# A gated attention and mixture-of-experts block on one core: the first batch's softmax in a written-out order over six banks, its values by way of DRAM, and the mixture's transposes moved up

## The chip, the core and the metric

One core of a Trainium2 chip runs the whole program. The metric is the device time of one execution, in microseconds (us). Five engines work side by side, each through its own instruction stream in order: TensorE (PE, matmuls, with its weight loads PEld), VectorE (DVE), ScalarE (ACT), GpSimd (POOL) and SyncE (SP, which issues DMAs). Nothing overtakes within a stream, so an instruction that waits holds up all behind it.

## The reference, cut to what matters

```python
# x: (8, 256, 512), ctx: (8, 256, 512); H = 32 heads of D = 16, HK = 8 key heads
x = x + tanh(g_xattn) * attention(layernorm(x), ctx)
x = x + tanh(g_ffn) * ffn(layernorm(x))

# attention: queries from [ctx, x]; keys and values from ctx and from x, side by side
q  = heads(concat([ctx, xn]) @ Wq);  k = heads(xn @ Wk);  sk = heads(ctx @ Wsk)
scores = q @ concat([sk, k]).T / 4 + alibi;  a window of 64 positions back, else -inf
o = softmax(scores) @ concat([ctx @ Wsv, xn @ Wv]);  return o @ Wo

# ffn: per token a softmax router over 128 experts, the best 4, each a mixture of 8 bases
basis = silu(xt @ w_gate) * (xt @ w_up)            # 8 bases of 256
out   = sum over the 4 experts of coeff * (mix[expert] . basis) @ w_down
out   = out + (silu(xt @ sw_gate) * (xt @ sw_up)) @ sw_down
```

## The kernel before

The eight batches follow each other, two tiles of 128 tokens each, all in float32. For a batch b there are four kinds of work, each a Python generator that records a few instructions and then yields an estimate of their time. `run` (near the end of the kernel) always advances the generator that is due first, so each engine's order is the order of recording.

- `project(b)` normalizes x, transposes it (`tr_x`, copied to `xnT` by ACT) and makes keys (`pk`, L491, copied to `kT` at L498), queries (`pq`, L510, copied to `qT` at L517) and values (`pv`, L530, copied into the padded tile `vpad` at L453). All of these take turns on the one PSUM bank with the tag "one", with `hold` and `give`.
- `diagonals` (L447) spreads `vpad` with 16 DMAs of 128 KB into the block-diagonal tile `vbd`, 2.1 MB in rows of 1 KB, which the matmuls with the softmax's result read.
- `attention(b)` has 16 steps u, two for each of 8 groups i. `score(i)` (L574) makes four score banks; in each step `soften` (DVE, L587) adds the bias and takes the minimum, `exponentials` (ACT, L601) follow, `divide` (reciprocal on DVE at L610, four multiplications on POOL at L613) and `turn` (a DVE transpose into `pt`, L621). After every two groups `values` (L643) multiplies `pt` by `vbd` and `take` (ACT, L660) copies the result to `oT`. `tail(b, t)` then makes the output projection (`po`, L763), the second normalization (`tr_f`) and the router (`pl`, `pst`, `pc`).
- `feed_forward(b)` multiplies ten pieces k (eight bases and two halves of the shared part) by a scheme with seven products of half size (`m`, L896 and L905). For that it needs sums of weight quarters: they are made once (`sub`, L848), stored to DRAM (`keep`, L852) and reloaded for later batches. For k = 0 to 3 `first_weights` makes them ahead of the first batch's feed-forward, on POOL; for the others `feed_forward(0)` makes them as it goes. At the end the mixture `mixed` is transposed (`pm`, L1067), copied (`mT`, L1070) and multiplied by `w_down` (`pd`, L1042).

Before the loops stand the loads and, in `project_first`, batch 0's first keys and queries: context keys, first-half queries, the transposes of x, then second-half queries. The rest of batch 0's projection, the values among it, is recorded by the same generator between steps of `attention(0)`. The setup runs under the framework's own ordering, what follows under the written one:

```python
        start(attention(0), 0.42, at=-0.62, total=74.1)
        start(first, 0.12, at=-0.615, total=7.1)
        start(project(1), 0.54, at=-0.54, total=44.0)
        start(first_weights(), 0.42, at=-0.52, total=25.0)
        start(once(coefficients, *coef_in), 1.0, at=-0.46)
```

Of the kernel before, what the change touches and what calls it, by code (L numbers as in the profile page):

```python
# [32 lines left out]
MASKED = 1e32  # L33


@with_exitstack
def gated_block(
# [38 lines left out]

    turns = [0]
# [15 lines left out]
    def hold():  # L93
        me = object()
        queue.append(me)
        while queue[0] is not me or now[0] < given[0] + GAP:
            yield 0.4
# [8 lines left out]
    def load(b):  # L106
        xt = three.tile([P, NT, HID], F32, tag="x", name=f"x_{b}")
        nc.sync.dma_start(xt, x[b].rearrange("(t p) d -> p t d", p=P))
        return xt

    def load_context(b):

        ctT = one.tile([P, NC, T], F32, tag="shT" if b == 1 else "ctT", name=f"ctT_{b}")
        nc.sync.dma_start(ctT, context_t[b].rearrange("(c p) t -> p c t", p=P))
        return ctT
# [8 lines left out]
    ctT_0 = load_context(0)  # L124
    wsk_sb = weight(wsk, HID, HK * D, "wsk", nc.scalar)
    for t in range(NT):
        nc.sync.dma_start(x_0[:, t, :], x[0, t * P : (t + 1) * P, :])
    loaded[0] = x_0, ctT_0
    wq_sb = const.tile([P, 2 * NC, HID], F32, tag="wq", name="wq")
    for half, eng in enumerate((nc.scalar, nc.sync)):  # L130
        if half:
            wk_sb = weight(wk, HID, HK * D, "wk", nc.scalar)
        eng.dma_start(
            wq_sb[:, half * NC : (half + 1) * NC, :],
            wq[half * HID : (half + 1) * HID].rearrange("(c p) n -> p c n", p=P),
        )
    wsv_sb = weight(wsv, HID, HK * D, "wsv", nc.scalar)
    wv_sb = weight(wv, HID, HK * D, "wv", nc.sync)
    loaded[1] = load(1), load_context(1)


# [3 lines left out]
    nc.gpsimd.memset(neghalf, -0.5)  # L145

# [26 lines left out]
    def transposed(dst, src, t, name, bank):  # L173
# [7 lines left out]
    first_normed = [norm(loaded[0][0], [t], f"a0_{t}")()[0] for t in range(NT)]  # L181

    rows_i = const.tile([P, 1], I32, tag="rows_i", name="rows_i")
    nc.gpsimd.iota(rows_i, pattern=[[0, 1]], base=0, channel_multiplier=1)
    odd_i = const.tile([P, 1], I32, tag="odd_i", name="odd_i")
    nc.vector.tensor_scalar(
        odd_i, rows_i, D, D.bit_length() - 1, op0=ALU.bitwise_and, op1=ALU.logical_shift_right
    )  # L190
    kmask = const.tile([P, 2], F32, tag="kmask", name="kmask")
    nc.vector.tensor_copy(kmask[:, 1:2], odd_i)
    nc.vector.tensor_scalar(
        kmask[:, 0:1], kmask[:, 1:2], -1.0, 1.0, op0=ALU.mult, op1=ALU.add
    )

# [20 lines left out]
    for kv in range(HK):  # L217
        nc.gpsimd.tensor_scalar(
            nbias[:, kv], dist, slope, 2.0 ** (-8.0 * G * kv / H), op0=ALU.mult, op1=ALU.mult
        )  # L220


    vpad = const.tile([P, NT * 2, (2 * HK + 1) * D], F32, tag="vpad", name="vpad")
    nc.gpsimd.memset(vpad.rearrange("p a n -> p (a n)"), 0.0)


    vbd = const.tile([P, P // Q, NT * 2, HK, 2 * D], F32, tag="vbd", name="vbd")

# [22 lines left out]

    def first_weights():

        for k in (2, 3, 0, 1):
            for g in range(1, 5):
                load_gu(k, g)
            if k == 2:
                yield 1.0
                later["wd"] = weight(w_down, I, HID, "wd", nc.sync)


                later["sd"] = sd = const.tile([P, NSI // 2, HID], F32, tag="sd", name="sd")
                nc.sync.dma_start(
                    sd, sw_down.rearrange("(j o p) n -> o p j n", o=2, p=P)[1]
                )
            if k == 3:
                yield 2.0
                yield from first_sums(2)
                yield 1.0
                yield from first_sums(3)  # L270
        yield 3.0
# [19 lines left out]
    def coefficients(amp, escale):  # L291
# [3 lines left out]
        nc.gpsimd.tensor_tensor(psq, amp, amp, ALU.mult)  # L295
        nc.gpsimd.tensor_tensor(mix, psq[:, :, 0], psq[:, :, 1], ALU.add)
# [56 lines left out]
    AFTER, BEFORE = 1.8, 0.8  # L353
    projected = {}
# [3 lines left out]
    def project_first():  # L358
# [38 lines left out]

        pk = early("pk_0", 2)
        keys(pk, 0, slice(0, T))
        pqs = [next_bank(f"pq_0_{g}")[:, 0, :P] for g in range(G - 1)]  # L400
# [4 lines left out]
        transposed(xnT, first_normed[0], 0, "x0", lambda shape, name: early(name, NC))()  # L405
# [3 lines left out]
        put_keys(pk, 1, tiles[0])  # L409
        for g in range(G):  # L410
            put_queries(pqs[g], g, 0)
        projected[0] = kT, qT
        yield 0.0
        evict = transposed(
            xnT, first_normed[1], 1, "x0",
            lambda shape, name: next_bank(name).rearrange("p t (a n) -> p (t a) n", n=P),
        )
        yield 0.5
        evict()
        pk = next_bank("pk_0_1")  # L420
        keys(pk, 1, tiles[1])
        yield 0.6
        put_keys(pk, 1, tiles[1])
        pv = next_bank("pv_0").rearrange("p t (s n) -> p t s n", s=2)
        for t in range(NT):
            for s, (w_sb, src) in enumerate(((wsv_sb, ctT), (wv_sb, xnT))):
                for c in range(NC):
                    nc.tensor.matmul(
                        pv[:, t, s, :], lhsT=src[:, c, tiles[t]], rhs=w_sb[:, c, :],
                        start=(c == 0), stop=(c == NC - 1),  # L430
                    )
            yield 1.0
        put_values(pv)
        for qd in range(P // Q):
            diagonals(qd, nc.sync if qd < 2 else nc.gpsimd)
        for g in range(G):
            pq = next_bank(f"pq_0_{g}_1")[:, 0, :P]
            queries(pq, g, tiles[1], range(2 * NC))
            yield 1.0
            put_queries(pq, g, 1)  # L440

    def diagonals(qd, eng):


        for g in range(G):
            at = D * (1 - g % 2)
            eng.dma_start(  # L447
# [10 lines left out]
    def project(b):  # L458
        def own():
            yield from hold()  # L460
# [11 lines left out]
        normed = norm(xt, range(NT), f"a{b}")  # L472
        yield 3.0
        xns = normed()
        yield 3.0
        xnT = two.tile([P, NC, T], F32, tag="xo", name=f"xnT_{b}")
        for t in range(NT):
# [11 lines left out]
        for s, (w_sb, src) in enumerate(((wsk_sb, ctT), (wk_sb, xnT))):  # L489
# [5 lines left out]
            yield AFTER  # L495
# [10 lines left out]
        for g in range(G):  # L506
            yield from own()
            pq = bank([P, T], f"pq_{b}_{g}")
            for c in range(2 * NC):
# [5 lines left out]
                if c % NC == NC - 1:  # L515
                    yield AFTER
# [10 lines left out]
        for t in range(NT):  # L527
# [6 lines left out]
            yield AFTER  # L534
# [5 lines left out]
    def attention(b):  # L540
# [17 lines left out]
        def bank(name):  # L558

            taken[0] += 1  # L560
            if b == 0 and taken[0] > 4 * NPAIR and taken[0] % 6 < 2:
                return other_bank(taken[0] % 6, name)
            return ps_sc.tile([P, 2 * COLS + P], F32, tag="sc", name=name)

        def score(i):

            par, qb0 = groups[i]
            scs = [bank(f"sc_{b}_{i}_{p}") for p in range(NPAIR)]
# [28 lines left out]

        def exponentials():
# [18 lines left out]
        def turn(u, pr, pt):  # L617

            qb = groups[u // 2][1] + u % 2
# [43 lines left out]

        n = len(groups)
        prs, dens, pts = {}, {}, {}
        for u in range(2 * n + 4):
# [10 lines left out]
            if i < n:  # L679
                prs[u] = three.tile([P, NPAIR, COLS], F32, tag="pr", name=f"pr_{b}_{u}")  # L680
                nmax = small.tile([P, NPAIR], F32, tag="nmax", name=f"nm_{b}_{u}")
                dens[u] = small.tile([P, NPAIR], F32, tag="den", name=f"dn_{b}_{u}")
            yield 1.0

            for step, ps in enumerate(((2,), (3,), (0, 1))):
                if b > 0 and u in (1, 2) and step < 2:
                    diagonals(2 * (u - 1) + step, nc.sync)
# [4 lines left out]
                if step == (0 if b > 0 else 1) and 0 <= u - 1 < 2 * n:  # L692
                    divide((u - 1) // 2, (u - 1) % 2, prs[u - 1], dens.pop(u - 1))
                if step == (1 if b > 0 else 2) and 0 <= u - 2 < 2 * n:
                    k = (u - 2) // 4
                    if (u - 2) % 4 == 0:
                        pts[k] = two.tile(
                            [P, P // Q, NPAIR, COLS], F32, tag="pt", name=f"pt_{b}_{k}"
                        )
                    turn(u - 2, prs.pop(u - 2), pts[k])  # L700
                if step == 1 and j == 1 and m is not None:
                    take(m, scs)
                    if m == n // 4 - 1:
                        start(tail(b, 0, oT), 0.30 if b > 0 else 0.22, total=37.0)
                if u < 2 * n + 2:
                    yield 1.0 if i < n else 0.8
        start(tail(b, 1, oT), 0.31 if b > 0 else 0.16, total=37.0)
# [159 lines left out]
    def feed_forward(b):  # L867
# [122 lines left out]
        for k in range(PIECES):  # L990
            late = b == 0 and k > 3
            more = b == 0 and 3 < k + 1 < PIECES
# [67 lines left out]
        four(last)  # L1060
        mix_product(last, 0)
        yield 0.86
# [5 lines left out]
        yield from second_gate(last)  # L1068
        mT = one.tile([P, NT, 2, P], F32, tag="mT", name=f"mT_{b}")
        nc.scalar.copy(mT, pm)  # L1070
        shared(po0, 0, 3, start=False, stop=False)
        yield 0.86
# [23 lines left out]
    EARLY, FIRST = -0.2, -0.04  # L1096
# [22 lines left out]
    with tc.manual_schedule():  # L1119


        first = project_first()
        next(first)
        coef_in = other_weights()
        start(attention(0), 0.42, at=-0.62, total=74.1)
        start(first, 0.12, at=-0.615, total=7.1)
        start(project(1), 0.54, at=-0.54, total=44.0)
        start(first_weights(), 0.42, at=-0.52, total=25.0)
        start(once(coefficients, *coef_in), 1.0, at=-0.46)
        at = -0.2  # L1130
        while 0 not in sides:
            at += 0.005
            run(at)
        for b in range(B):
            if b > 0:
                run(b + EARLY)
                if b + 1 < B:
                    start(attention(b + 1), 0.86, at=b + EARLY, total=74.1)
                run(float(b))
                at = float(b)  # L1140
            else:
# [44 lines left out]
```

## Time and profile before

| | |
|---|---|
| median of 3 runs | 1041.03 us (1040.71 to 1043.25) |
| the profiled execution's own time | 1039.15 us |
| its span, first to last instruction | 1037.4 us |
| PE busy | 990.9 us, 96% of the span |
| DVE, POOL, ACT busy | 601.5, 470.7, 442.0 us |
| mean granted PE clock | 0.988 |
| first feed-forward matmul (L896) | 104.8 us |
| from one batch's last store issued to the next's (239.8, 364.8, 487.6, 610.7) | 122.8 to 125.0 us |

The profile page gives each engine's busy share in 40 equal slices of 25.9 us, the clock that PE was granted in tenths, the chain of work that ended last, and the costliest groups of instructions. Other views are cut from the same trace: waits (who waited for whom), a timeline of one engine, and windows, a table of busy time in stretches. A matmul's row has pieces that overlap, so a group's length is read from the start of one group to the start of the next. "sc" is a score bank (and takes the values too), w the feed-forward weights, s their stored sums.

### The profile page before, as it was taken

Reading aid. Unit: us, or ns where it says so; the run is one execution under the profiler, and the core shown is the slowest. Engines: PE = TensorE matmul, PEld = TensorE weight load, DVE = VectorE, ACT = ScalarE, POOL = GpSimd, SP = SyncE. Lnnn points to the kernel's source line nnn. Section 1 sums busy time; section 2 is a strip of 40 time slices with the busy share of each in tenths; the row PEclk is TensorE's granted clock in tenths of the full one; section 3 lists DMA queues with packets and bytes.
Section 4 is the critical chain, followed back from the end, with each engine's and each line's share of the span. In section 5 each row is a group of like instructions: output and inputs, shape, how many; then the busy total and the mean of one; then the engine's idle time right before and its main releaser. Section 6 shows DMA issues by size and latency. Waiting matters only on the chain.

```text
span 1037.4 us, 27827 instructions
## 1 busy us (share of the span) xinstructions
PE 990.9 (96%) x10456; PEld 795.2 (77%) x10456; DVE 601.5 (58%) x2237; ACT 442.0 (43%) x1656; POOL 470.7 (45%) x896
## 2 busy tenths in 40 slices
PE   6779989999999999999999999999999999999998
PEld 5657868867888688886878868787788868776885
DVE  1555666767563685536755467545656467655453
ACT  2453454436542464425543255423554246431231
POOL 3666457735543264423634146432455325551341
PEclk9879999999999999999999999999999999999999
DMA  8733864579544694557745586455854468564891
GB/s 254 188 116 136 221 198 143 166 220 284 159 141 143 193 307 124 161 152 195 266 142 152 166 239 209 136 171 165 265 181 134 154 177 253 191 195 146 275 297 64
DMA packets 118311, 194.00 MB, mean 187 GB/s; under 512 B 12960, under 2 KB 34976, under 8 KB 118176
## 3 DMA queue, kind: packets, MB, share of 16 engines
q1 hardware_dynamic: 115680, 189.33, 59.4%
q10 hardware_dynamic: 2112, 1.84, 0.6%
q8 instruction: 83, 1.36, 0.5%
q0 software_dynamic: 384, 1.05, 0.5%
q14 instruction: 52, 0.43, 0.1%
HBM read 160.70 MB, written 14.68 MB: 169 GB/s over the span
## 4 chain that ended last, share of the span: by engine, by line
PE 79%; DVE 9%; DMA 4%; ACT 3%; POOL 2%; issue 2%; SPq 1%; ACTq 0%; POOLq 0%; DVEq 0%
PE m L896 31%; PE m L905 9%; PE pq L510 8%; PE sc L643 5%; PE po L763 5%; PE pd L1039 5%; PE sc L574 4%; PE pk L491 3%; PE pv L530 2%; PE pd L1042 2%; DVE pr L587 2%; PE pl L793 1%; DMA vbd<-vpad 1%; ACT pr L601 1%; POOL w L848 1%
## 5 line engine op out<-in xcount | busy, mean ns | idle before, releaser
L613 POOL TENSOR_SCALAR pr<-pr,rd 128x192 f32<-128x192 f32 (+2 forms) x512 | 209.6, 427 | 245.9 <-DVE rd L610 245.4
L601 ACT ACTIVATE pr<-pr,nm 128x192 f32<-128x192 f32 (+2 forms) x512 | 219.0, 431 | 108.5 <-DVE nm L587 65.6
L896 PE MATMUL m<-w,sT 128*128 128x256 f32 x1024 | 252.1, 380 | 0.1
L587 DVE CUSTOM_DVE_ANT_1 pr<-sc,nbias 128x192 f32<-128x192 f32 (+2 forms) x512 | 154.1, 322 | 124.0 <-PE sc L574 109.2
L896 PEld LDWEIGHTS m<-w,sT 128*128 128x128 f32 x1024 | 193.7, 190 | 27.4 <-issue 1.0
L896 PE MATMUL m<-w,hT 128*128 128x256 f32 x768 | 203.0, 387 | 1.0 <-DVE u L941 1.0
L896 PEld LDWEIGHTS m<-w,hT 128*128 128x128 f32 x768 | 139.0, 190 | 25.4 <-issue 6.5
L986 POOL TENSOR_TENSOR mixed<-mixed,th 128x256 f32<-128x256 f32 x112 | 81.7, 730 | 133.9 <-DVE th L981 133.9
L621 DVE STREAM_TRANSPOSE pt<-pr 128x768 f32<-128x768 f32 (+2 forms) x128 | 111.4, 871 | 4.3 <-POOL pr L613 2.4
L601 ACT ACTIVATION_READ_ACCUMULATOR pr<-pr,nm 128x1 f32 x512 | 97.9, 191 | 0.0
L942 POOL TENSOR_TENSOR m<-m,u 128x256 f32<-128x256 f32 x80 | 59.9, 749 | 83.6 <-DVE u L941 76.0
L858 ACT ACTIVATE th<-m 128x256 f32<-128x256 f32 x80 | 30.9, 386 | 142.8 <-DVE up L952 140.7
L643 PEld LDWEIGHTS sc<-pt,vbd 64*32 64x32 f32 x5120 | 61.6, 107 | 27.5 <-issue 13.2
L643 PE MATMUL sc<-pt,vbd 64*32 64x96 f32 (+2 forms) x5120 | 70.4, 230 | 7.9 <-DMA vbd<-vpad 4.3
L858 ACT ACTIVATE th<-gate 128x256 f32<-128x256 f32 x80 | 33.2, 415 | 94.2 <-DVE gate L964 94.2
L574 PE MATMUL sc<-kT,qT 32*128 32x192 f32 (+2 forms) x1024 | 66.2, 343 | 6.6 <-DVE nm L587 6.2
L952 DVE TENSOR_TENSOR up<-u,m 128x256 f32<-128x256 f32 x80 | 33.3, 416 | 67.0 <-PE m L896 42.2
L574 PEld LDWEIGHTS sc<-kT,qT 32*128 32x128 f32 x1024 | 46.1, 188 | 32.5 <-DVE nm L587 13.8
L964 DVE TENSOR_TENSOR gate<-u,m 128x256 f32<-128x256 f32 x80 | 33.2, 415 | 64.1 <-PE m L896 55.6
L905 PE MATMUL m<-sT,w 128*128 128x128 f32 x512 | 65.1, 275 | 0.0
L1039 PE MATMUL pd<-sd,shT 128*128 128x512 f32 x128 | 62.3, 610 | 1.6 <-DVE shT L975 1.6
L905 PEld LDWEIGHTS m<-sT,w 128*128 128x128 f32 x512 | 61.2, 192 | 0.2
(128 smaller groups left out, 1373.1 us busy)
## 6 DMA issues: line engine op xcount, KB each, us to landing
w<-s SPq DMA_DIRECT2D x288, 256.0 KB, 3.4
w<-in_L_ffn_w_gate SPq DMA_DIRECT2D x132, 256.0 KB, 3.2
w<-in_L_ffn_w_up SPq DMA_DIRECT2D x74, 256.0 KB, 4.1
vbd<-vpad SPq DMA_DIRECT2D x120, 128.0 KB, 3.1
s<-w SPq DMA_DIRECT2D x40, 256.0 KB, 3.2
w<-in_L_ffn_shared_w_gate SPq DMA_DIRECT2D x32, 256.0 KB, 2.8
w<-in_L_ffn_shared_w_up SPq DMA_DIRECT2D x18, 256.0 KB, 3.8
ctT<-in_ctx SPq DMA_DIRECT2D x8, 512.0 KB, 5.4
```

The lines of the kernel that those rows point to most:

```text
L510: nc.tensor.matmul(pq, lhsT=wq_sb[:, c, g * P : (g + 1) * P], rhs=(ctT if c < NC else xnT)[:, c % NC, :], start=(c == 0), stop=(c == 2 * N ...
L574: nc.tensor.matmul(seen(scs[p][:, j * COLS : (j + 1) * COLS], qb), lhsT=qT[rows, qb].rearrange("p g q -> p (g q)"), rhs=kT[rows, par, :, f ...
L587: nc.vector.tensor_tensor_reduce(out=part, in0=seen(scs[p][:, j * COLS : (j + 1) * COLS], qb0 + j), in1=bass.AP(tensor=bias.tensor, offset ...
L601: nc.scalar.activation(part, part, AF.Exp, bias=nmax, scale=-1.0, accum_out=den)
L613: nc.gpsimd.tensor_scalar(part, part, rden[:, p : p + 1], 1.0, op0=ALU.mult, op1=ALU.mult)
L621: nc.vector.transpose(pt[:, u % 4].rearrange("p c (s k) -> p (c s) k", s=2)[:, :, lo:], pr.rearrange("p c (s k) -> p (c s) k", s=2)[:, :, ...
L643: nc.tensor.matmul(scs[gp][32 * c : 32 * (c + 1), 2 * COLS + lo * Q : 2 * COLS + hi * Q], lhsT=vbd[rows, kb % (P // Q), kb // (P // Q) * 2 ...
L858: nc.scalar.activation(th, gate, AF.Tanh, scale=0.5)
L896: nc.tensor.matmul(dst, lhsT=sides_of[m][c], rhs=w[:, c, :], start=(first and c == 0), stop=(c == NC // 2 - 1), skip_group_check=True,)
L905: nc.tensor.matmul(dst[:, cols], lhsT=w[:, c, cols], rhs=sides_of[m][c], start=(first and ic == c == 0), stop=(c == NC // 2 - 1), skip_gro ...
L986: nc.gpsimd.tensor_add(mixed[t], mixed[t], th)
L1039: nc.tensor.matmul(po, lhsT=shT[:, ic, t * P : (t + 1) * P], rhs=down[ic], **flags)
```

## The change

1. **Loads.** x's second tile, the second half of `wq`, `wv`, and batch 1's x and context move from SP's queue to ACT's, in this order: `wsk`, first half of `wq`, `wk`, x's second tile, second half of `wq`, `wsv`, `wv`, batch 1's x and context. SP keeps the first context and x's first tile. The small weights (`other_weights`: gates, `wo`, `wr`) are loaded after the values' DMAs. Everything is now under the written order.
2. **Warm-up.** PE transposes `ident` 14 times into an unused bank, and ACT computes one tanh, which brings its table load forward.
3. **First batch.** `first_batch` replaces the loop of `attention(0)`: scores rotate over six banks (four "sc", two "gu"), `score(i+1)` is recorded half a group earlier, and the rest of batch 0's projection and all of batch 1's are recorded in fixed places (`piece`) instead of by due times.
4. **Values of batch 0.** `vpad` goes to a DRAM tile `vrows` in one DMA of 557 KB, and comes back to `vbd` in four of 512 KB, each to 32 partitions.
5. **Weight sums.** `first_weights` handles k = 2, 0, 1; k = 3 joins those that `feed_forward(0)` makes in its loop.
6. **Attention of batch 1** starts at -0.19 and is spread over 0.86 instead of 0.74.
7. **Mixture.** In each batch the four transposes `pm` are recorded ahead of the last piece's `four`, and the copy `mT` ahead of the last tanh (in `second_gate`).

```diff
+WARM = 14
-    for half, eng in enumerate((nc.scalar, nc.sync)):
...
+    load_queries(0)
+    wk_sb = weight(wk, HID, HK * D, "wk", nc.scalar)
+    nc.scalar.dma_start(x_0[:, 1, :], x[0, P:, :])
+    load_queries(1)
     wsv_sb = weight(wsv, HID, HK * D, "wsv", nc.scalar)
+    wv_sb = weight(wv, HID, HK * D, "wv", nc.scalar)
+    loaded[1] = load(1, nc.scalar), load_context(1, nc.scalar)
...
+    warm = const.tile([P, 1], F32, tag="warm", name="warm")
+    nc.scalar.activation(warm, neghalf[:, :1], AF.Tanh)
+    idle = next_bank("idle")
+    for _ in range(WARM):
+        nc.tensor.transpose(idle[:, 0, :P], ident, ident)
...
-        for k in (2, 3, 0, 1):
+        for k in (2, 0, 1):
...
+        def rest():
...
+            put_values(pv)
+            nc.sync.dma_start(
+                vrows.rearrange("p q a n -> q p (a n)"), vpad.rearrange("p a n -> p (a n)")
+            )
+            for g in range(G):
+                at = D * (1 - g % 2)
+                nc.sync.dma_start(
+                    vbd[g * Q : (g + 1) * Q].rearrange("p q a k r -> p q a (k r)"),
+                    vrows[:, :, :, at : at + 2 * HK * D],
+                )
...
+            yield from project(1, xns)
...
-            if b == 0 and taken[0] > 4 * NPAIR and taken[0] % 6 < 2:
-                return other_bank(taken[0] % 6, name)
+            if b == 0 and taken[0] % 6 in (5, 0):
+                return other_bank(int(taken[0] % 6 == 0), name)
...
+        def first_batch():
+            scs = {0: score(0)}
+            for u in range(2 * n + 3):
+                i, j = divmod(u, 2)
+                m = u // 4 - 1 if u >= 6 and u % 4 == 2 else None
+                if m is not None:
+                    into = scs.get(i - 1) or [bank(f"sc_{b}_{i}_{p}") for p in range(2)]
+                    values(m, 0, pts[m], into)
+                exponentials()
...
+                if m is None:
+                    piece(BEFORE, MORE)
+                yield 1.0
+                for step, ps in enumerate(((2,), (3,), (0, 1))):
+                    exponentials()
+                    for p in ps:
+                        if i < n:
+                            soften(i, j, p, scs[i], prs[u], nmax, dens[u])
+                    if step == 0 and m is not None:
+                        values(m, 1, pts[m], into)
+                        piece(BEFORE, MORE)
+                    if step == 1:
+                        if j == 1 and i + 1 < n:
+                            scs[i + 1] = score(i + 1)
...
+                        if m is not None:
+                            take(m, into)
...
-            late = b == 0 and k > 3
-            more = b == 0 and 3 < k + 1 < PIECES
+            late = b == 0 and k > 2
+            more = b == 0 and 2 < k + 1 < PIECES
...
-        four(last)
-        mix_product(last, 0)
-        yield 0.86
 
         pm = next_bank(f"pm_{b}").rearrange("p t (j n) -> p t j n", j=2)
         for t in range(NT):
             for j in range(2):
                 nc.tensor.transpose(pm[:, t, j, :], mixed[t][:, j * P : (j + 1) * P], ident)
-        yield from second_gate(last)
+        four(last)
+        yield 0.7
         mT = one.tile([P, NT, 2, P], F32, tag="mT", name=f"mT_{b}")
         nc.scalar.copy(mT, pm)
+        mix_product(last, 0)
+        yield 0.6
         shared(po0, 0, 3, start=False, stop=False)
-        yield 0.86
+        yield from second_gate(last)
         mix_product(last, 1)
...
-    EARLY, FIRST = -0.2, -0.04
+    EARLY, FIRST = -0.2, -0.19
...
+    project_first()
+    start(attention(0), 0.38, at=-0.585, total=70.0)
+    start(after_diagonals(), 0.2, at=-0.535, total=1.0)
+    start(first_weights(), 0.34, at=-0.537, total=18.0)
+    start(attention(1), 0.86, at=FIRST, total=74.1)
```

The engines' orders that come out of it, read from the two built programs: on PE the score group `sc_3` is followed by all matmuls of the first values, then the last second-tile queries of batch 0 (`pq_3`), a transpose of batch 1's x, and `sc_4`. On ACT the copies `oT` of those values and the copy of `pq_3` stand between the second and the third exponential of step 6. On SP the DMAs of `w_2`, `wo` and the other weights stand behind the values' DMAs. Pieces of batch 1's projection that take turns on the "one" bank stand back to back on PE in four places (each `pq` after the one before, `pv` after the last) where something stood between them.

## The prediction

> **What bounds the kernel now.** I read the 40 slices first: where is PE, the busiest engine, not busy?
>
> ```profile
> PE   6779989999999999999999999999999999999998
> PEclk9879999999999999999999999999999999999999
> ```
>
> Only in the first four or five slices of 25.9 us. In windows PE is busy 82.03 us of the first 104.8 (to the first feed-forward matmul), 121.3 of the next 127.2, and 116.6 of a later stretch of 117.0. So the start holds nearly all there is to win, and later only single waits. The waits of PE up to 104.8 us name the rest (us in total, times, longest):
>
> ```profile
> PE pk L373 <- DMA wsk<-in_L_xattn_Wsk: 5.6, 1, 5.6
> PE sc L574 <- DVE nm L587: 4.1, 4, 1.1
> PE sc L643 <- DMA vbd<-vpad: 2.3, 1, 2.3
> PE pq L386 <- DMA wq<-in_L_xattn_Wq: 2.2, 1, 2.2
> PE pk L491 <- ACT xnT L179: 2.0, 1, 2.0
> PE pq L510 <- ACT kT L498: 2.0, 1, 2.0
> ```
>
> And windows of 2 us show a second loss (stretch, length, then busy time of PE, PEld, DVE, ACT, POOL; granted clock, DMA share, GB/s):
>
> ```profile
> 38.00:40.00 2.00, 2.00 (x20) 2.00 (x20) 0.82 (x1) 0.93 (x5) 2.00 (x5) 1.00 1.10 212
> 44.00:46.00 2.00, 0.24 (x2) 0.03 (x1) 0.00 (x0) 0.55 (x4) 1.39 (x4) 1.00 1.05 235
> 46.00:48.00 2.00, 1.41 (x48) 1.34 (x49) 0.31 (x3) 0.00 (x0) 0.00 (x0) 0.52 1.05 385
> 58.00:60.00 2.00, 2.00 (x6) 1.64 (x5) 0.43 (x1) 0.66 (x4) 2.00 (x5) 0.50 0.35 131
> ```
>
> PE waits for vbd from 44.2 to 46.6, and from then to about 63 its clock is half; the same at 12 to 15.4 after the wait for wq. While vbd is moved (38 to 40) all DMA engines are busy at only 212 GB/s; weights move at 385 (46 to 48). The wait itself, in PE's timeline (start, length, what; in brackets the idle time before it):
>
> ```profile
> 43.92 0.32 PE L643 MATMUL sc<-pt,vbd 64*32 64x96 f32 x2 [0.58 <-DVE rd L610]
> 46.59 1.03 PE L643 MATMUL sc<-pt,vbd 64*32 64x96 f32 x46 [2.35 <-DMA vbd<-vpad]
> ```
>
> From the first third on, each of the later batches shows one wait of its own (PE's waits after 150 us):
>
> ```profile
> PE pd L1042 <- ACT mT L1070: 5.0, 6, 1.0
> ```
>
> **The change, part by part.** I walk PE's order, since the end follows it, with durations from this execution. Weight work and streams at full clock: a query half (8 instructions of 128x256) 1.8, scores 0.87, a value group 2.2, po 3.5, four transposes 0.6.
>
> *Start to the first scores (before: 22.9).* The first half of wq lands at 11.2 behind some 3.2 MB at 376 GB/s; in the new order only 2.1 MB stand before its end: about 8.3. The transpose of x's first tile now precedes it (normalized at 8.8, the rows BATCH_NORM to xn take 2.6 us from x's landing at 6.3; POOL's mask work before its power takes 3.3 us and is done by 5). So the queries begin at 9.4. The 14 transposes (0.22 each cold) lie in the 5.6 us wait for wsk and cost nothing; they should spare the half clock, so the first-half queries take 3.7 instead of 5.5. Then transpose, keys, second halves: 0.6, 1.0, 3.7. Scores at 18.4, a gain of 4.5. If the clock is half anyway: 20.4. ACT's added DMA issues (nine of about 0.5 us) end by 7 and its table load at 8.3, before the keys need it.
>
> *To the first values.* Values' projection 3.6, so vpad is copied at 23.4 (before 32.2). DVE sets the pace meanwhile: steps 2 to 5 are 4 x 0.28 plus reciprocal plus a turn of 0.44 to 0.87, with batch 1's statistics (1.9) and normalization (1.2) among them; `pt` is complete at 33.9, and PE has done sc_3 by 33.
>
> *The DRAM trip (no row shows it).* Write: stores s<-w of 256 KB land in 2.0 to 5.8 us, median 3.2; for 557 KB I take 4. SP waits for it, then issues four loads of 512 KB: the first at 27.6, flowing 1.5 us later. At 385 GB/s 2.1 MB take 5.4 us, at the 212 of the vbd rows 10. vbd lands at 35 to 41; I take 38, nearer the vbd rows, since these loads go to 32 partitions too. So PE waits some 4 us, and the wait that I see removed at 46.6 is moved to 38, not gone. Behind it on PE stand pq_3 and sc_4; on ACT two exponentials of step 6, so DVE's reciprocal and POOL behind them; on SP the loads of w_2, wo, wr. Those are wanted at 42 (w_2, by POOL) or later than 55, and cover it.
>
> The clock: a wait of 2.35 us brought half clock here, so 4 us will. Under half clock PE then has values, pq_3 and a transpose, 4.6 us of work, of which about 2 are added until the clock returns (3.3 us in the first case). sc_4 starts at 38 + 4.6 + 2 = 44.6 (before: mostly 51.9, and under half clock to 63).
>
> The Trainium skill's page "TensorE: Matmul & The Clock Gate" (section on the HAM clock gate) gives about 3.4 us of idleness as what halves the clock; this trace had it after 2.35. By the page a landing at 36 would keep the clock full and sc_4 would come at 40.6; by the row, at 42.6. Against the trip speaks the page "DMA: Bandwidth & Descriptors" (anatomy of one DMA): most of a DMA's fixed cost is the receipt of the last write, heaviest for DRAM; by its 2.0 us plus bytes / 436 GB/s I would estimate the write at 3.3 us. Neither changes the sum here.
>
> *To the first feed-forward matmul (before 104.8).* Work in PE's new order from sc_4 on: five score groups 4.2, three value groups 6.6, three transposes 1.8, keys 3.5, eight query halves 14.4, two po 7.1, two pl 2.0, values 3.6, router 0.4: 43.6. Waits: the xnT copy (now behind sc_4's own exponentials) 2.0 as before, kT 2.0 as before, the four back-to-back pieces on the "one" bank 0.65 each (a copy of 0.38, its queueing): 2.6; tail 1.2 (xn_f 0.5, hT 0.7). Together 8; bounds 3 (the copies keep up) and 11 (each behind two exponentials of 0.45). Softmax is covered: POOL, its slowest, has 10 x 1.62 + 8 sums x 1.27 + 0.6 = 27 us, to about 72, while PE reaches the last values near 79. First feed-forward matmul: 44.6 + 43.6 + 8 = 96.2. By then 2.4 us are done (half of pv, sc_0) that before come after it: comparable 93.8. **Gain 11.0**, bounds 5 and 20.
>
> *Feed-forward of batch 0.* Batch 1's diagonals are issued earlier on SP: two waits for vbd (2.0) and a 0.7 wait on xnT may go; I take 2.5. The sums for k = 3 now run in the loop: 1.6 us of DVE, 2.6 of POOL, four stores on SP ahead of later loads. k = 4 to 7 do this already and PE waits for no weight there, so I cost it at nothing; without cover it is one landing, 3 us. Attention of batch 1 starting earlier moves work, not PE's amount. Bounds -1 and 4.
>
> *Mixture.* The copy mT waited behind gate (0.42) and tanh (0.42) of the last piece. In its new place pm ends, then PE has `four` (0.9) and one `shared` (0.43), 1.3 us over a copy of 0.57. Of the 5.0 us I take 4.0 (an exponential of 0.45 may still stand before it on ACT); bounds 2 and 5. New wait: pm needs mixed 0.9 us earlier; POOL finished that sum nearly 10 us ahead in the last batch. The silu of the last tile comes later, and PE has 3.4 us of matmuls before it is needed against 2.
>
> **Sum.** 11.0 + 2.5 + 4.0 = 17.5. The profiled execution: 1039.15 - 17.5 = 1021.65; the median stands 1.88 above it (1041.03): 1023.5.
>
> **Rivals.**
>
> 1. *The trip is in time.* At 385 GB/s vbd lands near 35, PE waits about 1 us and keeps its clock, sc_4 comes at 39.6, 5 earlier; with waits of 4 instead of 8, gain 20; total 26.5: 1014.5. For it: 385 in the weight rows, and DRAM as source. Against: 212 wherever 32 partitions are written by the vbd rows.
> 2. *PE's new waits eat the start.* The "one" bank's pieces back to back and ACT's copies behind exponentials cost 11, vbd comes at 41: gain 5, nothing in the feed-forward, 3 from the mixture: 8, so 1033. For it: the two 2.0 rows, both ACT copies that gate that bank.
> 3. *Slower: the trip stops the queue.* values stands ahead of pq_3 and sc_4 in PE's stream, so each us after 38 costs one. With a margin of 17.5 + 3.1, it decides from a landing at 58.6, 35 us after vpad's copy; at 62 the time is 1047.5. Against: the longest vbd landing was 9.3 us, the longest store 5.8.
> 4. *It changes nothing that counts:* softmax on POOL and DVE, not PE, sets the first 100 us, so the start moves only its 4.5 and gives it back at PE's later waits, and the mT wait turns into one on ACT's queue: 1039 to 1043. For it: POOL is busy 9.0 and 9.2 of 10 us at 50 to 60 and 80 to 90. Against: in the same start POOL sits idle 20 us for DVE's reciprocals, and DVE 23 for PE's scores.
>
> **Chances.** Forecast (1017 to 1030) 0.57, the trip in time 0.14, waits eat 0.17, nothing 0.06, slower 0.06. Below 0.3% (3.1 us) this measurement can't tell a change: faster 0.88, same 0.06, slower 0.06. The range takes in the first two rivals and the bounds of the unknown terms, 1013 to 1034; what is left out is nothing, slower, and the edges of the others.
>
> **What would show it.** Right: sc_0 near 18.4; four vbd<-vrows landing near 38; a PE wait of some 4 us there, half clock for 3 to 5 us and not 16; first feed-forward matmul near 96; the mT row under 1 us; batch 0's feed-forward without a vbd wait. Wrong: vbd landing before 34 or after 42; PE's waits between 45 and 96 far from 8 us; a wait on w in batch 0's pieces; later batches, 122.8 to 125.0 us from store to store before, changed by other than the mixture's 0.3 to 0.6 us.

## Result and the profile after

| | before | after | ratio, 95% interval |
|---|---|---|---|
| median of 10 runs each, us | 1039.14 | 1047.72 | 1.0073 (1.0048 to 1.0098) |
| profiled execution: time, span, us | 1039.15, 1037.4 | 1045.74, 1043.9 | |

The change makes the kernel slower by some 8 us; 1023.5 was forecast. By places, from the two traces (span 6.5 us longer; 2.4 us of PE's work has moved ahead of the first feed-forward matmul):

| stretch | before | after | difference | forecast |
|---|---|---|---|---|
| to the first feed-forward matmul | 104.8 | 108.9 | +4.0, comparable +1.6 | -11.0 |
| from there to batch 0's last store | 135.0 | 138.3 | +3.4, comparable +5.8 | -2.5 |
| the rest | 797.6 | 796.7 | -0.9 | -4.0 |

The 40 slices of the page show both places: PE's slice 2 (25.9 to 51.8 us) reads 4 where it read 7, and slice 6 (130 to 156 us), in batch 0's feed-forward, 7 where it read 8.

```profile
PE   8489979999999999999999999999999999999998
PEclk9799989999999999999999999999999999999999
```

Among PE's waits up to the first feed-forward matmul one entry now stands out (us in total, times, longest), and the wait of SP, which issues the DMAs, for the write of vpad stands behind it:

```profile
PE sc L716 <- DMA vbd<-vrows: 14.9, 2, 10.0
PE pq L571 <- ACT kT L559: 1.7, 1, 1.7
PE pk L552 <- ACT xnT L205: 1.6, 1, 1.6
```

```profile
SPq L464 <- DMA vrows<-vpad: 10.7, 1, 10.7
```

PE's timeline shows how the 14.9 us fall (start, length, in brackets the idle time before): sc_3 is done at 34.5, then nothing.

```profile
33.32 1.22 PE L637 MATMUL sc<-kT,qT 32*128 32x192 f32 x16
44.58 0.50 PE L716 MATMUL sc<-pt,vbd 64*32 64x96 f32 x2 [10.05 <-DMA vbd<-vrows]
49.91 2.33 PE L716 MATMUL sc<-pt,vbd 64*32 64x96 f32 x125 [4.83 <-DMA vbd<-vrows]
```

And the windows (the last three columns: granted clock, DMA share, GB/s) say what the DMA engines did meanwhile. The write of vpad to DRAM was issued at 24.6; in its time the engines are a quarter busy. The loads, issued from 36.1 on, have them all busy at 190 to 243 GB/s, with the clock at half from 38.2 to 55.3.

```profile
26.00:28.00 2.00, 2.00 (x19) 1.76 (x18) 1.93 (x7) 1.67 (x8) 1.15 (x4) 1.00 0.24 63
30.00:32.00 2.00, 2.00 (x21) 2.00 (x20) 1.74 (x11) 1.79 (x10) 1.68 (x5) 1.00 0.27 87
38.00:40.00 2.00, 0.00 (x0) 0.00 (x0) 0.00 (x0) 0.00 (x0) 0.00 (x0) 0.55 1.06 243
42.00:44.00 2.00, 0.00 (x0) 0.00 (x0) 0.00 (x0) 0.00 (x0) 0.00 (x0) 0.50 1.12 203
```

In batch 0's feed-forward the two vbd waits of before are gone, but DVE now waits for a weight, and PE for DVE, both in the timeline (DVE's line, then PE's; the clock is half from 134 to 141):

```profile
130.87 0.69 DVE L960 TENSOR_TENSOR w<-w,w 128x512 f32<-128x512 f32 x1 [2.19 <-DMA w<-in_L_ffn_w_up]
```

```profile
135.91 1.55 PE L716 MATMUL sc<-pt,vbd 64*32 64x96 f32 x64 [4.93 <-DVE nm L650]
```

From 150 us on there is no row for mT any more (before: 5.0 us in 6). In its place stands this one, 0.3 us at a time before and 1.6 now:

```profile
PE sc L637 <- DVE nm L650: 8.0, 6, 1.6
```

### The profile page after: what moved, and what is told of

It reads as the page before. It is cut to its first block, busy times and chain, and to the rows that moved or that the text cites. A ratio compares the mean times of both kernels' runs of the same rounds, so it can differ in the third digit from the quotient of the medians.

```text
span 1043.9 us, 27803 instructions
## 1 busy us (share of the span) xinstructions
PE 992.4 (95%) x10470; PEld 798.4 (76%) x10470; DVE 602.8 (58%) x2241; ACT 441.6 (42%) x1657; POOL 466.2 (45%) x884
## 4 chain that ended last, share of the span: by engine, by line
PE 81%; DVE 10%; DMA 4%; ACT 3%; issue 1%; POOL 0%; SPq 0%; DVEq 0%; ACTq 0%
PE m L1008 32%; PE m L1017 9%; PE pq L571 9%; PE sc L716 6%; PE po L875 5%; PE pd L1151 4%; PE sc L637 4%; PE pk L552 2%; PE pv L591 2%; PE pd L1154 2%; DVE pr L650 2%; ACT pr L669 2%; DMA vbd<-vrows 1%; DMA vrows<-vpad 1%; PE pq L403 1%
## 5 line engine op out<-in xcount | busy, mean ns | idle before, releaser
L1008 PEld LDWEIGHTS m<-w,sT 128*128 128x128 f32 x1024 | 194.2, 191 | 27.4 <-issue 0.5
L716 PE MATMUL sc<-pt,vbd 64*32 64x64 f32 (+2 forms) x5120 | 69.8, 231 | 22.4 <-DMA vbd<-vrows 14.9
L637 PE MATMUL sc<-kT,qT 32*128 32x192 f32 (+2 forms) x1024 | 63.9, 336 | 9.1 <-DVE nm L650 8.6
L1151 PE MATMUL pd<-sd,shT 128*128 128x512 f32 x128 | 65.1, 634 | 0.7 <-DVE shT L1087 0.7
```

The source lines that it names most:

```text
L637: nc.tensor.matmul(seen(scs[p][:, j * COLS : (j + 1) * COLS], qb), lhsT=qT[rows, qb].rearrange("p g q -> p (g q)"), rhs=kT[rows, par, :, f ...
L716: nc.tensor.matmul(scs[gp][32 * c : 32 * (c + 1), 2 * COLS + lo * Q : 2 * COLS + hi * Q], lhsT=vbd[rows, kb % (P // Q), kb // (P // Q) * 2 ...
L1008: nc.tensor.matmul(dst, lhsT=sides_of[m][c], rhs=w[:, c, :], start=(first and c == 0), stop=(c == NC // 2 - 1), skip_group_check=True,)
L1151: nc.tensor.matmul(po, lhsT=shT[:, ic, t * P : (t + 1) * P], rhs=down[ic], **flags)
```

## Experiments

Three places lost time, so three theories: the trip by DRAM is slow because its one write runs on few DMA engines; the sums of k = 3 lost their cover; the mixture's wait only changed its name. In what follows "1040" is the time of the kernel before, whose median was 1040.3 to 1041.9 beside these runs; ratios are to it, with their 95% intervals.

**The write in four pieces (e1_four_writes).**

```
-nc.sync.dma_start(vrows.rearrange("p q a n -> q p (a n)"), vpad...)      # 4 x 32 x 1088
+for qd in range(P // Q):                                                # 32 x 1088 each
+    nc.sync.dma_start(vrows[:, qd]..., vpad[qd * Q : (qd + 1) * Q]...)
```

> The changed kernel with its one write of the padded values to DRAM (4 x 32 x 1088) cut into four writes of 32 x 1088, one per quadrant; the DRAM tile and the four loads stay. Theory A (the one write, whose outermost dimension has 4 entries, runs on a quarter of the DMA engines: 0.18 to 0.27 of their time, 48 to 87 GB/s): the writes are issued at 24.6 to 27.3, land by 31 instead of 35.3, the loads are issued from 31 and vbd lands at 36 to 43 instead of 44.6 to 49.9; PE's waits for vbd fall from 14.9 us to 5 to 9, and the time by 6 to 10 us, to 1036 to 1042 on the scale on which the changed kernel is 1047.7 and before 1039.1. Theory B (the trip to DRAM is slow by itself, by its receipt or by the 32 source partitions): the last write still lands 10 us after the first is issued, vbd after 44, time within 2 us of the changed kernel's. Theory C (softmax on DVE and POOL sets the first 100 us, not vbd): vbd lands early, but the first feed-forward matmul stays at 107 to 109.

Measured: 1041.23, ratio 0.9993 (0.9972 to 1.0014), so 8 us faster than the changed kernel. Each write landed 2.2 us after its issue (median); the loads were issued at 27.4 instead of 36.1, and the values began at 36.5 instead of 44.6, the last of vbd at 42.1 instead of 49.9. Windows of this run:

```profile
24.00:26.00 2.00, 2.00 (x20) 2.00 (x20) 2.00 (x11) 2.00 (x10) 1.24 (x4) 1.00 0.73 174
30.00:32.00 2.00, 2.00 (x20) 2.00 (x19) 2.00 (x7) 1.60 (x9) 1.79 (x4) 1.00 1.13 215
```

The same bytes now take the engines at 0.73 and 174 GB/s: theory A. The Trainium skill has the rule that the prediction should have weighed: its page "DMA: Bandwidth & Descriptors" (section on why a DMA increments its semaphore by 16 and not by 1) says that a DMA issued from SP runs on the largest number of engines up to 16 that divides the slowest dimension of both sides. For 4 x 32 x 1088 that makes 4 of 16; the row's 0.18 to 0.27 agrees with it, and 32 x 1088 makes 16. No row shows on how many engines a single one of the four writes ran.

**No trip (e2_no_dram).**

```
-nc.sync.dma_start(vrows..., vpad...)
-for g in range(G): nc.sync.dma_start(vbd[...], vrows[...])
+for qd in range(P // Q):
+    diagonals(qd)                      # 16 DMAs of 128 KB, as before, all on SP
```

> The changed kernel with vbd filled straight from vpad by the 16 DMAs of before, all on SP, in place of the write and the four loads by way of DRAM. Theory A (what was lost in the start is the trip): 16 issues of some 0.6 us from 24.6 to 34.5, the last landing 4 to 9 us later, at 38 to 43 (before it took 14.4 us from the copy of vpad to the end of PE's wait), against 49.9 with the trip; PE's wait 3 to 8 us instead of 14.9, first feed-forward matmul at 98 to 102 instead of 108.9, time 6 to 10 us below the changed kernel's. Theory B (the slow part is writing 32 partitions of vbd, whatever the source): vbd after 46, gain under 4 us. Theory C (softmax sets the start): wait gone, first feed-forward matmul within 2 us of 108.9.

Measured: 1033.62, 0.9928 (0.9903 to 0.9952): 15 us (0.0145 x 1040) below the changed kernel. Waits for vbd are 2.1 us in all, sc_4 starts at 42.5, the first feed-forward matmul at 96.2. Each DMA landed 2.4 us after its issue (before: 5.4 to 6.3 on two queues at once). Theory A, with more gain than the 6 to 10 us that it gave: the last values wait for vbd until 37.2, where e1 has them at 42.1, so the trip costs even with fast writes. The first feed-forward matmul comes when the prediction had it, by another way: the trip was not needed for it.

**The sums of k = 3 ahead again (e3_k3_ahead).**

```
-for k in (2, 0, 1): ...          # first_weights;  late = b == 0 and k > 2
+for k in (2, 3, 0, 1): ...       # and yield from first_sums(3);  late = b == 0 and k > 3
```

> The changed kernel with the sums of the weights of k = 3 made ahead of batch 0's feed-forward again, as in the kernel before (loaded in the order 2, 3, 0, 1). Theory A (DVE's 2.2 us wait for w_3 stands ahead of the softmax of batch 1, and from it come PE's 4.9 us wait at 131 to 136 and the half clock to 140): both waits go, the time falls by 4 to 8 us, to 1040 to 1044. Theory B (the wait comes from SP, which carries batch 1's diagonals ahead of the weights, and only moves to k = 4): a DVE wait of 1 to 3 us on w_4 appears one piece later (near 142), with a PE wait behind it, and the time stays within 2 us. Both: nothing changes before 75 us, where vbd is still late.

Measured: 1046.00, 1.0044 (1.0023 to 1.0066), 3 us below the changed kernel, at the edge of what can be told. The 4.9 us wait went, but a wait for a weight came in its place, now PE's own:

```profile
133.81 1.13 PE L1010 MATMUL m<-w,sT 128*128 128x256 f32 x4 [2.43 <-DMA w<-in_L_ffn_w_up]
```

and before the first feed-forward matmul PE waits 1.6 us for rrd and 1.3 for xn_f, which the extra sums delay. Neither theory as put; A's causes are right, its price too high.

**The mixture's order alone (e4_mixture_only), and the changed kernel without it (e5_old_mixture).**

```
 shared x2, first_tile(last)
-four(last); mix_product(last, 0); pm; second_gate(last); mT
+pm; four(last); mT; mix_product(last, 0); shared; second_gate(last)    # on the kernel before (e5: undone on after)
```

> The kernel before with the mixture's new order alone. Theory A (the wait for mT was not the last thing to end: DVE's router work and softmax set when the next batch's second group of scores can be written, and PE waits there for what it no longer waits for mT): the waits for mT go (5.0 us in 6), the wait of the second score group for the softmax grows from 0.3 to some 1.6 us in each of five batches (+6 us in all), time within 0.2% of before. Theory B (the reorder is worth its 4 us, and the later batches of the changed kernel are slowed by something else, the order in which the score banks are taken above all): waits for mT go, the scores' wait stays at 0.3, time 4 us below before (1035).

> The changed kernel with the mixture's order of before. Theory A (the new order costs the 5.7 us that it cost alone: it turns 0.96 us of waiting for mT and 0.31 us for the scores' bank into one wait of 1.57 us, and a wait of that length halves PE's clock for some 3.4 us in a part of the batches): the waits for mT come back (5 us in 6), the scores' wait falls from 8.6 to under 3 us, PE's clock is full from 150 us on but for one place at most, and the time is 4 to 7 us below the changed kernel's, at 1041 to 1044 where before is 1040. Theory B (in the changed kernel the mixture's order costs nothing, since DVE's softmax of the next batch sets the batches either way): within 2 us of the changed kernel.

Measured: alone 1046.16, 1.0045 (1.0020 to 1.0070): slower by 5 us, where one theory said nothing and the other 4 us faster. Undone on the changed kernel: 1046.81, 1.0041 (1.0021 to 1.0061), 3 us faster than it with overlapping intervals. The waits moved as theory A said; its sum was wrong, because the new wait costs more than its row. First before, then the new order alone, at the same place of PE's timeline:

```profile
352.94 0.59 PE L574 MATMUL sc<-kT,qT 32*128 32x192 f32 x4
353.85 1.12 PE L574 MATMUL sc<-kT,qT 32*128 32x192 f32 x12 [0.32 <-DVE nm L587]
354.90 2.84 PE L1039 MATMUL pd<-sd,shT 128*128 128x512 f32 x6
```

```profile
354.27 0.59 PE L574 MATMUL sc<-kT,qT 32*128 32x192 f32 x4
356.43 1.22 PE L574 MATMUL sc<-kT,qT 32*128 32x192 f32 x12 [1.57 <-DVE nm L587]
357.58 4.40 PE L1039 MATMUL pd<-sd,shT 128*128 128x512 f32 x6
```

The last line of each: the same six matmuls take 2.84 and 4.40 us. The wait of 1.57 us had halved the clock; in this trace it did so in four of five batches, in the changed kernel's in two of five. The Trainium skill's page "TensorE: Matmul & The Clock Gate" (section on the HAM clock gate) puts the threshold at a window of some 3.4 us, free-running, so that a loss depends on its phase; the dependence on the phase agrees, the length does not: 1.57 us was enough here. The traces show the phase. All changes in their clock records lie on a grid of 3.41 us. In the five profiles that have this wait (e4, the changed kernel, e1, e2, e3: 25 waits) the clock halved behind the 12 waits of which at least 1.43 us fell into one stretch of the grid, and behind none of the 13 that the grid cut so that at most 1.38 us did.

**The router's work behind the softmax (e9_router_after, on the changed kernel; e12_before_router, on the kernel before).** DVE's timeline in the changed kernel names what PE waits for until 483.79: nine router operations, from 481.48 to 483.45, stand ahead of the two that write the last `nm` and so free the scores' bank (the first and the last of the nine, then the two):

```profile
481.48 0.16 DVE L920 RECIPROCAL rrd<-rdn 128x1 f32<-128x1 f32 x1
483.37 0.16 DVE L933 RECIPROCAL rts<-tsum 128x1 f32<-128x1 f32 x1
483.45 0.27 DVE L650 CUSTOM_DVE_ANT_1 pr<-sc,nbias 128x128 f32<-128x128 f32 x1
483.65 0.28 DVE L650 CUSTOM_DVE_ANT_1 pr<-sc,nbias 128x128 f32<-128x128 f32 x1
```

```
+if b > 0 and t == 1:
+    yield 2.0
 rden = small.tile([P, 1], F32, tag="rrd", name=f"rrd_{n}")
```

> The changed kernel with one yield of 2.0 ahead of the router's nine operations on DVE (second tile, later batches), which puts them behind the two softmax operations that free the scores' bank instead of ahead of them. Theory A (those 1.8 us of DVE work are what PE waits for in the mixture): the scores' wait of 1.57 us in five batches falls under 0.4, PE's clock stays full from 150 us on, and of 5 x 1.57 plus some three half-clock stretches of 1.7 us the time gets most back: 7 to 13 us below the changed kernel, 1035 to 1041 where before is 1040. Theory B (PE only arrives earlier at the next thing that DVE owes it, shT or the next batch's softmax): the wait moves to another row, time within 3 us of the changed kernel.

> The kernel before with the router's operations behind the softmax and nothing else. Theory A (there PE waits 0.96 us for mT ahead of the 0.31 us for the scores' bank, and only the second is DVE's): mT's 5 us stay, the scores' waits go (1.6 us), time 0 to 3 us below before. Theory B (what the move frees on DVE lets tanh, and so mT, come earlier): mT's wait falls too, 5 to 8 us below before.

Measured: on the changed kernel 1033.09, 0.9918 (0.9891 to 0.9946): 16 us faster than without, where 7 to 13 was expected. On the kernel before 1031.74, 0.9910 (0.9881 to 0.9939): 9 us, where theory A gave 0 to 3 and theory B 5 to 8; mT's wait stayed (5.2 us in 7), so neither holds as put. From 150 us on the scores' wait is 0.3 us in all in the one and has no row in the other, and the clock is full in every mixture of both. One mixture of e9, then one of e12:

```profile
480.66 1.33 PE L637 MATMUL sc<-kT,qT 32*128 32x192 f32 x16
481.91 2.84 PE L1153 MATMUL pd<-sd,shT 128*128 128x512 f32 x6
```

```profile
353.83 0.93 PE L574 MATMUL sc<-kT,qT 32*128 32x192 f32 x16
354.69 2.84 PE L1041 MATMUL pd<-sd,shT 128*128 128x512 f32 x6
```

From the scores' start to the next group it is 1.25 us in e9 and 0.86 in e12, against 1.96 in the kernel before (352.94 to 354.90), 3.22 in the changed kernel and 3.31 in e4 (354.27 to 357.58). So the row of "0.32 idle" in the kernel before cost 1.1 us: the two parts of the group that it cuts are busy 0.59 and 1.12 us, the whole group 0.93. This accounts for most of both gains. Between the last stores of batch 1 and batch 6, e9 is 13.5 us shorter than the changed kernel (599.1 to 585.5): five groups at 2.0 and two half-clock stretches at 1.7 make 13.3. e12 is 8.0 us shorter than the kernel before (597.1 to 589.1): five groups at 1.1, and a wait of 1.6 us for shT in batch 6 that went as well, make 7.1; the half clock that stood behind that wait went with it.

**All together (e10_all_three, e8_two_and_old, e11_two_fixes, e13_sum_later).** No trip and the router's move, with k = 3 ahead (e10) or in the loop (e11); e8 is e10 with the old mixture and no router's move; e13 is e11 with the first sum of k = 3 ten DVE instructions later:

```
-if more: sub(k + 1, 1)            # ahead of batch 1's statistics
+if more and k + 1 > 3: sub(k + 1, 1)
 ...
+if k + 1 == 3: sub(k + 1, 1)      # next to sub(k + 1, 3)
```

> The changed kernel without the trip by DRAM (vbd straight from vpad, as in the run that gave 1033.6), with the sums of k = 3 made ahead again, and with the router's operations behind the softmax. If the three causes are separate, their gains add: 1047.7 - 14 (trip) - 3 (sums) - 7 to 13 (mixture) = 1018 to 1024. If the mixture's and the sums' gains are covered by something common (softmax on DVE): 1028 to 1033.

> The same as the last, but with the mixture's order of before in place of the router's move: 1047.7 - 14 - 3 - 4 to 7 = 1024 to 1027 by theory A (the mixture's new order costs 4 to 7 us and nothing more is to be had there); below the run with the router's move, if that move gives less than 4 us.

> The changed kernel without the trip by DRAM and with the router's operations behind the softmax; the sums of k = 3 stay in the loop as changed (the run with all three gave 1022.1). Theory A (making those sums ahead of batch 0's feed-forward costs in the start what it saves in the loop: in the profiles it brings PE waits of 1.5 us for rrd and 1.3 us for xn_f before the first feed-forward matmul, which comes 2.5 us later, and a wait of 2.7 us for w in place of one of 5.2 for nm): within 3 us of 1022. Theory B (the step of the sums costs 4 to 8 us, as first thought): 1026 to 1030.

> The run before (no trip, router behind) with one DVE operation moved: the first sum of k = 3 goes from ahead of batch 1's statistics to behind them, next to the third, 10 DVE instructions later. Theory A (DVE's 2.5 us wait for w_3 is what makes PE wait 5.2 us for nm near 120, and the clock halve after it): DVE's wait falls under 0.5, PE's wait to 1 to 3 us, the half clock near 124 goes: 4 to 7 us below the run before it, some 1014 to 1018. Theory B (w_3 arrives too late for any order, since its buffer comes free only after k = 1): the same wait one place later, gain under 2 us.

| | median, us | ratio, 95% interval |
|---|---|---|
| e10: all three | 1022.11 | 0.9825 (0.9795 to 0.9854) |
| e8: no trip, k = 3 ahead, old mixture | 1036.43 | 0.9956 (0.9937 to 0.9975) |
| e11: no trip, router's move | 1019.57 | 0.9789 (0.9761 to 0.9818) |
| e13: and the sum later | 1018.45 | 0.9769 (0.9736 to 0.9802) |

Trip and mixture are separate: the ratio of the changed kernel less what e2 and e9 gained by themselves (1.0073 - 0.0145 - 0.0155) is 0.9773, and e11 has 0.9789. e10 lies in the range expected, but by luck: that range had 7 to 13 us for the mixture, and with the measured 16 and e3's 3 the sum would be 0.9744, where e10 has 0.9825. e8 misses by 10 us: k = 3 ahead is no gain without the trip, since it delays the start (first feed-forward matmul at 98.7 in e10 and 101.7 in e8, against 94.9 in e11 and 96.2 in e2), and the old mixture keeps its mT waits (5.9 us in 7) and scores' waits. e11, within 3 us of e10, agrees with theory A there: in the loop the sums cost no more than ahead of it. e13 gains 1 us by the medians, less than its interval and than the 4 to 7 expected: PE's wait falls from 5.3 to 3.4 us only, because the third sum now waits for the weight, 1.1 us, which is nearer theory B. e13 is the fastest kernel of this study: 24 us (21 to 27) below before.

**Is the mixture's new order worth anything, once DVE is out of the way? (e15_best_old_order: e13 with the old order; e16_before_both: e12 with the new.)**

> The kernel that gave 1018.5 (no trip, router behind, first sum later) with the mixture's order of before. Theory A (with DVE out of the way the mT wait is the last thing to end, and the new order saves it): the waits for mT come back, some 5 us in 6, and the time rises by 3 to 6 us, to 1021 to 1025. Theory B (PE then waits for tanh and silu of the last tile in either order): within 1.5 us of 1018.5.

> The kernel before with the router's operations behind the softmax and the mixture's new order as well; with the old order that gave 1031.7. Theory A: 3 to 6 us less, 1026 to 1029, no row for mT and the scores' wait under 0.4 us. Theory B: within 1.5 us of 1031.7.

Measured: e15 1023.37, 0.9830 (0.9802 to 0.9859), against 0.9769 for e13: the new order gives 6 us (theory A). e16 1030.56, 0.9896 (0.9864 to 0.9928), against 0.9910 for e12: 1.5 us, not to be told from nothing. The traces, from batch 1's last store to batch 6's, give 590.4 to 586.2 us (4.2) for the first pair and 589.1 to 587.8 (1.3) for the second. So with DVE out of the way the new order gains 4 to 6 us in the one kernel; in the other a gain isn't shown.

**The warm-up (e14_no_warm_up, a single run).** e11 with WARM = 0.

> The kernel with two fixes (no trip, router behind) without the 14 transposes that keep PE busy while it waits for wsk. Theory A (they keep the clock from half at 12 to 15): the clock reads 0.5 for some 3 us there again, the first half of the queries takes 5.3 to 5.5 us instead of 4.2, sc_0 comes 1 to 2 us later (19.4 to 20.4 instead of 18.4). Theory B (it was the wait for wq, which is gone, that halved the clock): clock 1.0 throughout, sc_0 within 0.3 us of 18.4.

Measured: no clock under 1.00 shows from 8 to 18 us (the record begins at 10.5, see the end), and sc_0 comes at 19.25 instead of 18.48. Neither theory as put: what goes is the speed of the first matmuls. First without, then with the 14 transposes:

```profile
5.57 3.78 PE L387 MATMUL pk<-ctT,wsk 128*128 128x256 f32 x8 [5.57 <-DMA wsk<-in_L_xattn_Wsk]
```

```profile
5.65 1.99 PE L389 MATMUL pk<-ctT,wsk 128*128 128x256 f32 x8 [1.04 <-DMA wsk<-in_L_xattn_Wsk]
```

It is 1.8 us on the keys, and 0.8 at sc_0, as with the fast keys x's transpose waits 1.1 us for xn_a. And it is not certain: of the eleven profiles with the transposes seven show the keys at 2.0 us and four, the changed kernel's own among them, at 3.8. The five without them (e14, and the four with the start of before) show 3.4 to 3.8.

## Why the prediction was wrong

*Start to the first scores: right.* sc_0 at 19.4 in the profile of after, 18.4 to 18.7 in most of the others with the transposes, forecast 18.4. Its cause was half wrong: the clock at 12 to 15 is full without the transposes too (e14). That it is kept because the wait for wq is gone fits, and was not tested by itself.

*The DRAM trip: the step that failed first.* The write was put at 4 us by stores of 128 rows. It took 11.5 us from its issue (24.6) to the first load's (36.1), 10.7 of them SP's wait: one DMA with a slowest dimension of 4, while four of 32 rows landed in 2.2 us each (e1). The 3.3 us that the prediction estimated by the page "DMA: Bandwidth & Descriptors" were further off; the page gives that figure for DMAs issued from GpSimd, and this one was issued from SP. The loads took 13.8 us from the first issue to the last use, where 10.4 was taken and 13.4 was the bound. So vbd was complete at 49.9 instead of 38 (7.5 us of it the write, 3.4 the loads, 1.0 the later issue), PE waited 14.9 us instead of 4, and the clock was half for some 17 us instead of 3 to 5. This is rival 3's mechanism, at its price: 11.9 us after 38 take away the start's gain of 11.0 (measured: +1.6). That its example, 1047.5 for a landing at 62, is the measured time is luck.

*From sc_4 on: right.* 52.2 us from sc_4 to the first feed-forward matmul (forecast 43.6 + 8 = 51.6); the waits in it were the named ones. With vbd at 37 (e2) that matmul came at 96.2, which is the forecast; that it is so exact is luck, since sc_4 started at 42.5 instead of 44.6 and the way from there took 53.8 instead of 51.6.

*Feed-forward of batch 0: failed.* The vbd waits went, as forecast. The sums of k = 3 "costed at nothing", on the ground that k = 4 to 7 do the same: but w_3's loads are issued on SP from 124.4 to 127.7 only, behind batch 1's 16 diagonals, a load of x and one of the context (from 106.7 on), so DVE waited 2.2 us, PE 4.9, and the clock halved. SP also waited there for PE to give weight buffers back (3.4 us in 4, from 116 to 131); what each of the two adds was not separated. Even the bound without cover, 3 us, was too low, as it counted the landing and not the queue behind DVE or the clock.

*Mixture: the wait went, the gain did not.* The prediction asked what else stands ahead of the copy on ACT, and named pm and silu as new waits. It did not ask what PE meets next: the scores' bank, freed by DVE behind nine router operations. That wait stood in the trace of before at 0.3 us, because the mT wait covered it. The gain comes only once that is moved, and its size, 4.0, stays open (e15: 6; e16: 1.5, not to be told from nothing).

*Rival 3 had 0.06.* It was given a landing at 58.6 as the point from which it decides, with the other two terms as its margin. These failed too, so a landing at 50 was enough.

## What to carry to other kernels

Before a wait is counted as gain, follow the waiting engine to its next instruction and ask what frees that one's buffers: a wait may be the cover of another. A transfer's price is read from rows of its own shape, the slowest dimension above all, not from rows of its size. And price a wait on PE by the distance between the starts of the groups around it, the half clock after it included, not by its idle time alone.

## What the runs showed of the hardware

- PE's clock can halve after a wait of 1.57 us (four of five in one trace, two of five in each of four others); each such loss took 1.6 to 1.7 us from the matmuls behind it. Whether it does depends on where the wait lies on the grid of 3.41 us: with 1.43 us or more in one stretch it did, with 1.38 or less it didn't.
- A clock of 1.00 in the first microseconds says nothing: the record has no entry there, and a window without one prints 1.00. The first entry, full clock, begins at 4.2 to 5.3 us in the seven profiles whose first keys took 2.0 us, and at 8.5 to 15.0 us in the nine in which they took 3.4 to 3.8.
- In each of the twelve profiles with the changed start PE makes one long stop, between 193 and 215 us, in the middle of a group of 96 small matmuls, for 2.4 to 4.0 us, and the waits name nothing that releases it. Behind nine of these stops, with 1.88 us or more in one stretch of the grid, the clock was half for 3.4 to 6.8 us; behind three (e1, e2, e3, with 1.76 or less) it stayed full. So the limit isn't the 1.4 us of the mixture's waits. In the kernels with the start of before such stops took 0.3 to 1.8 us. In e11 and in e14, which has 14 PE transposes fewer ahead of it:

```profile
200.29 0.88 PE L708 MATMUL sc<-pt,vbd 64*32 64x96 f32 x37 [3.34 <-issue]
```

```profile
203.19 0.54 PE L706 MATMUL sc<-pt,vbd 64*32 64x64 f32 x23 [4.02 <-issue]
```

  37 matmuls of the group are left in the one and 23 in the other, just 14 fewer: the stop stands at a fixed count of PE's instructions. The DMA records tie it to the loading of instructions. They have a queue of the kind "instruction" with 83 transfers of 16 KB in each run, and in all sixteen profiles one of them ends 1.3 to 1.6 us before PE goes on after its longest such stop (e11: it runs from 197.9 to 198.8, PE goes on at 200.3). In the twelve it begins only after PE has stopped, by 0.2 to 1.6 us. Why it begins so late, and whether it waits behind the weights, isn't shown; the prediction had no term for it, and it is part of the 5.8 us of batch 0's feed-forward.
